# One-hot rows of j built token by token in a two-stage expert kernel

## The chip, the cores and the metric

The kernel runs on one core of a Trainium2 chip. The metric is the device time of one execution in microseconds (us). The engines are named as in the profile: PE is TensorE's matrix multiplication and PEld its weight load, DVE is VectorE, ACT is ScalarE, POOL is GpSimd, and SP issues most of the DMAs.

## What is computed

The reference is one layer on x of shape (2, 4096, 256): an attention-like part with running sums, and then an expert part whose choice of experts is made per token. Cut to the expert part:

```
s1 = einsum('bshd,nd->bshn', q1, K1);  s2 = einsum('bshd,nd->bshn', q2, K2)   # 8 heads, 64 keys each
v1, i1 = top_k(s1, 10);  v2, i2 = top_k(s2, 10)
vals, best = top_k(v1[..., :, None] + v2[..., None, :], 10)                # per head
expert_idx = (i1 * 64 + i2)[best]                                          # 0..4095
scores = softmax(vals)
h = einsum('bsd,bshkd->bshk', x, W_down[expert_idx])
h = gelu(h) * scores
out = einsum('bshk,bshkd->bsd', h, W_up[expert_idx])
```

Each token picks 8 x 10 = 80 experts among the first 4,096, with a weight for each.

## The kernel before, in words

The kernel doesn't gather the experts. It computes gelu(x W_down) for all 4,096 experts, multiplies it by a weight that is zero for an expert that was not picked, and multiplies the result with all of W_up. An expert's number is written as e = 32 j + c, with j from 0 to 127 (JE = 128) and c from 0 to 31 (EC = 32).

The work goes in 32 blocks of 256 tokens (16 stretches of each of the 2 sequences, in turn). A block's work has these parts:

- `attention`: the attention part of a block, with the norms, up to the queries qT.
- `scores` and `route`: for each half block of 128 tokens, the scores, the top 10 of each side and of their sums, the softmax, and the numbers j and c. They are packed into pk (five planes of 128 x 128 bf16: j, c, and three bf16 parts of the weight), and TensorE transposes the planes, so that a row is one of the 80 picks and a column is a token. ScalarE copies the result out of PSUM: plane j into `row`, and the other four into `rows`, each value repeated RUN = 4 times.
- `hidden`: the matmuls of x2T with the tiles wd (loaded by DMA), and on ScalarE their Gelu, which gives the tiles A (128 j x 32 c x 128 tokens).
- `weigh`: for each token, the weights of all 4,096 experts as a product of two one-hot matrices, and A times them. It is described below.
- `outputs`: the matmuls of A with the tiles wu into ps_acc, a norm, and the sum with x.

`weigh` takes 128 tokens in four builds of TS = 32 tokens. `build` makes on VectorE:

- hj, whether pick r of token t has this j. First, once per 128 tokens, `xj` holds j - 8m for m from 0 to 15 (a copy of `row` and four subtractions that double what is there). Then eight comparisons with the constants 0 to 7, of 16 x 32 elements each, fill hj. Its layout is (j, t): the 128 values of one token lie 32 elements apart.
- hc, whether pick r of token t has this c: one comparison of the constant `cols` (0 to 31) with rows, 32 x 32 elements. Its layout is (t, c).
- hw, hc times each of the three parts of the weight, 3 x 32 x 32 elements.

For each token TensorE then loads the token's 128 x 128 slice of hj as weights (`fl.tensor.ld`) and multiplies it with the token's three parts of hw, 32 columns each, into the token's 32 columns of ps_s (`fl.tensor.mm`, three times). The product of 16 tokens fills one of the two ps_s buffers, and VectorE multiplies A by it. Four tokens make one group in the order on TensorE, and behind each group one matmul of `outputs` of the half block before is put in, where there is one.

All engine operations are recorded first and issued later. `together` interleaves the streams (the experts of block n, the routes of block n+1, the attention of block n+2) by the numbers that they yield. `Flow.plan` then puts each engine's operations into a fixed order: it plays the program with a cost for each operation (`Flow.cost`), and takes on each engine the earliest recorded operation whose inputs are there by those costs. For VectorE a comparison with a constant of n bf16 elements costs n/4/0.96 + 68 ns there, and one of two bf16 tensors n/2/0.96 + 68 ns. The engines run these orders, with semaphores for what one needs of another. Since `emit` issues everything, the profile shows one line for nearly all operations: L404, with L403 for the weight loads of the one-hot product and of the transposes of pk and L401 for their matmuls. The tiles' names tell them apart.

Of the kernel before, what the change touches and what calls it, by code (L numbers as in the profile page):

```python
# [12 lines left out]
BF16 = mybir.dt.bfloat16  # L13
U16 = mybir.dt.uint16
AF = mybir.ActivationFunctionType
ALU = mybir.AluOpType
AX = mybir.AxisListType

P = 128
# [7 lines left out]
JE = 128  # L27
EC = NE // JE
R = 80
TS = 32  # L30
# [3 lines left out]
RUN = 4  # L34
# [381 lines left out]
def layer_kernel(  # L416
# [5 lines left out]
    nc = tc.nc  # L422
# [3 lines left out]
    fl = Flow(nc, tc, ctx)  # L426
    for tag, words in (
        ("ph", 512), ("tmp", 512), ("tmp2", 512), ("sinT", 512), ("cosT", 512), ("xn", 512), ("xT", 514), ("kc", 514),
        ("ks", 514), ("bh", 256), ("gate", 256), ("w0", 256), ("bl", 512), ("qT", 1024), ("v", 256), ("iu", 256),
        ("i1", 40), ("i2", 40), ("ci", 108), ("bv", 80), ("bu", 64), ("left", 8), ("right", 8), ("rsd", 2), ("hot", 1080),  # L430
        ("sm", 80), ("ssum", 8), ("ej", 80), ("rest", 80), ("xj", 1024),
    ):
        fl.ring(tag, words)
    for tag, words in (("st1", 6), ("mv1", 2), ("rs1", 1), ("st2", 12), ("mv2", 4), ("rs2", 2), ("x2T", 512),
                       ("s", 1024), ("hj", 2048), ("hw", 1536), ("hc", 512)):
        fl.ring(tag, words, 2)
    for tag, words in (("row", 64), ("rows", 1024), ("A", 4096), ("wd", 1024), ("wu", 1024)):
        fl.ring(tag, words, 3)
    fl.ring("xt", 512, 4)
    fl.ring("o", 256)  # L440
    for tag, words, bufs in (("mm", 512, 3), ("sc", 1024, 1), ("s", 512, 2), ("acc", 512, 1)):
# [3 lines left out]
    const = ctx.enter_context(tc.tile_pool(name="const", bufs=1))  # L445
# [1 line left out]

    ident = const.tile([P, P], F32, name="ident")
    make_identity(nc, ident)
    cols = const.tile([P, EC], BF16, name="cols")  # L450
    nc.gpsimd.iota(cols, pattern=[[1, EC]], base=0, channel_multiplier=0, allow_small_or_imprecise_dtypes=True)
    iota = const.tile([P, NCAND, RUN], BF16, name="iota")
    nc.gpsimd.iota(iota, pattern=[[1, NCAND], [0, RUN]], base=0, channel_multiplier=0,
                   allow_small_or_imprecise_dtypes=True)
# [40 lines left out]
    ps = fl.tile([1, D], F32, "ps_mm")  # L495
# [299 lines left out]
    def route(s):  # L795


        v = fl.tile([P, NH, 2, 16], F32, "v")
# [12 lines left out]
        i = 0  # L811
        while i < TOPK:
            w, n = WIDTHS[i], WIDTHS.count(WIDTHS[i])
# [45 lines left out]
        n = NCAND  # L859
        while n > 1:  # L860
            m = n // 2
# [5 lines left out]
        sm = fl.tile([P, NH, TOPK], F32, "sm")  # L867
        fl.vector.tensor_sub(sm, bv, bv[:, :, 0:1].to_broadcast([P, NH, TOPK]))
        fl.scalar.activation(sm, sm, AF.Exp)
        ssum = fl.tile([P, NH], F32, "ssum")  # L870
# [6 lines left out]
        ej = fl.tile([P, 2, R], U16, "ej")  # L877
# [4 lines left out]
        rest = fl.tile([P, NH, TOPK], F32, "rest")  # L882
# [7 lines left out]
        ps = fl.tile([P, 5, P], BF16, "ps_mm")  # L890
        with fl.group():
            for n in range(5):
                fl.tensor.ld(ps[:, n, :], pk[:, n, :], is_transpose=True)
                fl.tensor.mm(ps[:, n, :], pk[:, n, :], identb, start=True, stop=True, is_transpose=True)
        row = fl.tile([P, P], BF16, "row")
        rows = fl.tile([P, P // TS, 4, TS, RUN], BF16, "rows")
        fl.scalar.copy(row, ps[:, 0, :])
        fl.scalar.copy(rows.rearrange("p q n t u -> p n q t u"), ps[:, 1:5, :].rearrange("p n (q t) -> p n q t", t=TS)
                       .unsqueeze(4).to_broadcast([P, 4, P // TS, TS, RUN]))
        return row, rows  # L900

    def hidden(x2T):

# [31 lines left out]
    def weigh(A, rows, before):  # L935

        row, rows = rows
        xj = fl.tile([P, 16, P], BF16, "xj")  # L940
        fl.vector.tensor_copy(xj[:, 0, :], row)
        for s in (8, 4, 2, 1):
            v = xj.rearrange("r (a b s) t -> r a b s t", b=2, s=s)
            fl.vector.tensor_scalar(v[:, :, 1, 0, :], v[:, :, 0, 0, :], 8.0 * s, None, ALU.subtract)

        yield 3

        def build(t0):
            hj = fl.tile([P, JE, TS], BF16, "hj")
            for i in range(8):  # L950
                fl.vector.tensor_scalar(hj.rearrange("r (m j) t -> r m j t", j=8)[:, :, i, :],
                                        xj[:, :, t0 : t0 + TS], float(i), None, ALU.is_equal)
            hc = fl.tile([P, TS, EC], BF16, "hc")
            fl.vector.tensor_tensor(
                hc.rearrange("r t (a u) -> r t a u", u=RUN),
                cols.rearrange("r (a u) -> r a u", u=RUN).unsqueeze(1).to_broadcast([P, TS, EC // RUN, RUN]),
                rows[:, t0 // TS, 0].unsqueeze(2).to_broadcast([P, TS, EC // RUN, RUN]), ALU.is_equal,
            )
            hw = fl.tile([P, 3, TS, EC], BF16, "hw")
            fl.vector.tensor_mul(  # L960
                hw.rearrange("r n t (a u) -> r n t a u", u=RUN),
                hc.rearrange("r t (a u) -> r t a u", u=RUN).unsqueeze(1).to_broadcast([P, 3, TS, EC // RUN, RUN]),
                rows[:, t0 // TS, 1:4].unsqueeze(3).to_broadcast([P, 3, TS, EC // RUN, RUN]),
            )
            return hj, hw

        ready = build(0)
        yield 3
        for t0 in range(0, P, TS):
            hj, hw = ready  # L970
            if t0 + TS < P:
                ready = build(t0 + TS)
                yield 3
            for g in range(0, TS, TG):
                ps = fl.tile([P, TG, EC], F32, "ps_s")
                for t in range(0, TG, TU):
                    with fl.group():
                        for i in range(t, t + TU):
                            w = hj[:, :, g + i]
                            fl.tensor.ld(ps[:, i, :], w)  # L980
                            for n in range(3):
                                fl.tensor.mm(ps[:, i, :], w, hw[:, n, g + i, :], start=n == 0, stop=n == 2)
                    next(before, None)
                a = A[:, :, t0 + g : t0 + g + TG]
                fl.vector.tensor_mul(a, ps.rearrange("p t c -> p c t"), a)
                yield 1
        for _ in before:
            pass
        yield 1
# [16 lines left out]
    def routes(qT):  # L1006
        rows = []
        for s in scores(qT):
            rows.append((yield from route(s)))
        return rows  # L1010

    def experts(block, xt, A, rows, before, x2T):


        for j in range(NJ):
            yield from weigh(A[j], rows[j], before)
            before = outputs(*block, j, xt, A[j])
        A = None
        if x2T is not None:
            A = yield from hidden(x2T)  # L1020
        return A, before
# [7 lines left out]
    for n, block in enumerate(blocks):  # L1029
# [7 lines left out]
        A, before = ends[0]  # L1037
        x0 = x1
        if not last1:
            rows = ends[1]  # L1040
# [39 lines left out]
```

## Time and profile before

| | us |
|---|---|
| median of 3 runs (least to most) | 4083.58 (4077.91 to 4088.07) |
| the profiled execution | 4087.09 |
| its span, first to last instruction | 4085.3 |
| PE busy (share) | 3834.6 (94%) |
| DVE busy | 3735.9 (91%) |
| ACT busy | 1837.9 (45%) |
| POOL busy | 153.9 (4%) |

The profiled execution is 3.5 us above the median. Busy times of an engine are those of its operations, with overlaps counted once. Matmuls are pipelined, so a busy PE is not PE at its peak. The costliest groups of the product are 24,576 matmuls ps_s<-hw,hj (994.9 us busy), 8,192 weight loads of hj (963.9), 2,048 comparisons for hj (512.0), 256 products hw (446.0), 512 products A<-ps_s,A (346.7) and 256 comparisons hc (171.1). The first weight load of hj is at 194.6 us; before it the first blocks' attention, routes and hidden layer are made.

### The profile page before, as it was taken

The page shows a single profiled execution, that of the slowest core. Times are in us where ns is not written, and L with a number is a line of the kernel's source. Part 1 is how long each engine was busy: PE and PEld are TensorE (multiplying, and loading weights), DVE is VectorE, ACT ScalarE, POOL GpSimd, SP SyncE. Part 2 cuts the span into 40 slices and gives each one's busy share as a digit, 9 for nine tenths or more (in the row PEclk, how much of TensorE's full clock was granted, in tenths as well). Part 3 has the DMA queues.
Part 4 walks back from the last instruction along what each step waited for, and adds up shares of the span by engine and source line. Part 5 has one row for each costly group of instructions (what it writes and reads, how often), then busy time and mean ns, then how long its engine had stood idle before and what let it go on. Part 6 is the DMA issues. An engine that isn't in the chain of part 4 may idle for free.

```text
span 4085.3 us, 79868 instructions
## 1 busy us (share of the span) xinstructions
PE 3834.6 (94%) x36870; PEld 3300.2 (81%) x20486; DVE 3735.9 (91%) x17525; ACT 1837.9 (45%) x3251; POOL 153.9 (4%) x264
## 2 busy tenths in 40 slices
PE   3499999999999999999999999999999999999998
PEld 2388888888888888888888888888888888888887
DVE  3879999999999999999999999999999999999986
ACT  3344544444544444544444544444544444544431
POOL 0000000000000000000000000000000000000000
PEclk8699999999999999999999999999999999999989
DMA  5023333223333233333233333233333233333233
GB/s 205 29 93 120 106 115 123 90 96 127 101 116 125 89 100 124 106 115 123 91 96 127 100 117 125 89 100 124 98 122 122 90 98 126 103 115 125 86 108 121
DMA packets 145151, 447.83 MB, mean 110 GB/s; under 512 B 17777, under 2 KB 44146, under 8 KB 143730
## 3 DMA queue, kind: packets, MB, share of 16 engines
q1 hardware_dynamic: 139392, 440.46, 33.2%
q8 instruction: 225, 3.69, 0.4%
q10 hardware_dynamic: 5362, 2.28, 0.2%
q14 instruction: 172, 1.41, 0.1%
HBM read 425.90 MB, written 16.78 MB: 108 GB/s over the span
## 4 chain that ended last, share of the span: by engine, by line
PE 66%; DVE 31%; ACT 2%; ACTq 1%; issue 1%; DMA 0%; POOL 0%; POOLq 0%; SPq 0%
PE ps_mm L404 35%; PE ps_s L401 16%; PE ps_acc L404 12%; DVE hj L404 6%; DVE hw L404 4%; DVE hot L404 4%; PE ps_sc L404 3%; DVE ph L404 2%; DVE A L404 2%; DVE st L404 1%; DVE iu L404 1%; DVE hc L404 1%; DVE bl L404 1%; DVE v L404 1%; ACT rows L404 1%; DVE bu L404 1%
## 5 line engine op out<-in xcount | busy, mean ns | idle before, releaser
L404 PE MATMUL ps_mm<-x2T,wd 128*128 128x256 f32 x4096 | 1115.9, 423 | 44.2 <-ACT A L404 25.8
L403 PEld LDWEIGHTS <-hj 128*128 128x128 bf16 x8192 | 963.9, 141 | 103.2 <-DVE hw L404 29.0
L404 PEld LDWEIGHTS ps_mm<-x2T,wd 128*128 128x128 f32 x4096 | 854.0, 213 | 214.0 <-issue 81.9
L401 PE MATMUL ps_s<-hw,hj 128*128 128x32 bf16 x24576 | 994.9, 189 | 31.5 <-DVE hj L404 13.8
L404 PE MATMUL ps_acc<-wu,A 128*128 128x256 f32 x4096 | 1006.6, 393 | 6.9 <-DVE o L404 4.2
L404 PEld LDWEIGHTS ps_acc<-wu,A 128*128 128x128 f32 x4096 | 792.4, 197 | 123.5 <-DVE o L404 10.2
L404 ACT ACT_TABLE_LOAD x658 | 844.2, 1283 | 38.8 <-issue 26.0
L404 ACT ACTIVATE A<-ps_mm 128x256 f32<-128x256 f32 x1024 | 349.5, 383 | 976.3 <-PE ps_mm L404 961.3
L404 DVE TENSOR_SCALAR hj<-xj 128x512 bf16<-128x512 bf16 x2048 | 512.0, 302 | 0.0
L404 DVE TENSOR_TENSOR hw<-hc,rows 128x3072 bf16<-128x3072 bf16 x256 | 446.0, 1742 | 0.0
L404 DVE TENSOR_TENSOR A<-ps_s,A 128x512 f32<-128x512 f32 x512 | 346.7, 680 | 102.3 <-PE ps_s L401 62.4
L404 DVE FIND_INDEX8 iu<-v,s 128x8 uint32<-128x64 f32 x2048 | 428.1, 217 | 0.0
L404 DVE MAX8 v<-s 128x8 f32<-128x64 f32 x2048 | 374.3, 210 | 15.9 <-ACT s L404 15.9
L404 ACT ACTIVATE sm<-sm 128x80 f32<-128x80 f32 x64 | 17.3, 270 | 706.7 <-DVE sm L404 706.6
L404 DVE MATCH_REPLACE8 s<-v,s 128x64 f32<-128x64 f32 x1024 | 210.5, 208 | 0.0
L404 POOL CAST pk<-sm 128x80 bf16<-128x80 f32 x64 | 35.6, 556 | 3830.3 <-DVE sm L404 3830.3
L404 DVE TENSOR_TENSOR hc<-cols,rows 128x1024 bf16<-128x1024 bf16 x256 | 171.1, 678 | 0.0
L404 DVE MATCH_VALUE_LOAD iu<-v,s 128x8 f32 x2048 | 149.3, 73 | 0.0
L404 DVE RECIPROCAL rs<-rs 128x2 f32<-128x2 f32 (+1 forms) x160 | 22.3, 154 | 136.5 <-ACT rs L404 136.5
L404 PE MATMUL ps_mm<-x2T,wq 128*128 128x256 f32 x512 | 125.2, 388 | 1.0 <-ACT qT L404 0.6
L404 PE MATMUL ps_sc<-kbd,qT 128*128 128x256 f32 x512 | 124.8, 386 | 0.2 <-ACT qT L404 0.2
L404 PE MATMUL ps_mm<-xT,wg 128*128 128x256 f32 x512 | 122.3, 386 | 0.3 <-ACT tmp L404 0.3
(161 smaller groups left out, 4159.7 us busy)
## 6 DMA issues: line engine op xcount, KB each, us to landing
wu<-wu_d SPq DMA_DIRECT2D x512, 512.0 KB, 4.2
wd<-wd_d SPq DMA_DIRECT2D x256, 512.0 KB, 3.5
xt<-in_attn_x_dram SPq DMA_DIRECT2D x32, 256.0 KB, 2.9
A<-in_table_dram SPq DMA_DIRECT2D x8, 1024.0 KB, 7.2
out_dram<-o SPq DMA_DIRECT2D x64, 128.0 KB, 3.1
ph<-in_attn_pos_phases_dram SPq DMA_DIRECT2D x16, 256.0 KB, 3.9
wu_d<-A SPq DMA_DIRECT2D x8, 512.0 KB, 5.2
wd_d<-wd SPq DMA_DIRECT2D x8, 512.0 KB, 3.3
```

Source lines behind the costliest of these rows:

```text
L401: return engine.add_instruction(ins)
L403: return engine.ldweights(args[1], is_transpose=kw.get("is_transpose"), tile_position=(0, 0))
L404: return getattr(engine, op)(*args, **kw)
```

## The change

hj gets hc's layout, (t, j), so that the 128 values of one token are neighbours. It is made as hc is, by one comparison of two tensors: `cols`, which now counts to 127, against plane j of rows. So `rows` holds all five planes, in one ScalarE copy, and `row`, `xj` and its five operations per 128 tokens are gone. The weight load takes `hj[:, g + i, :]` in place of `hj[:, :, g + i]`. hw, hc, the matmuls and A's product are what they were.

```
-        row = fl.tile([P, P], BF16, "row")
-        rows = fl.tile([P, P // TS, 4, TS, RUN], BF16, "rows")
-        fl.scalar.copy(row, ps[:, 0, :])
-        fl.scalar.copy(rows.rearrange("p q n t u -> p n q t u"), ps[:, 1:5, :].rearrange("p n (q t) -> p n q t", t=TS)
-                       .unsqueeze(4).to_broadcast([P, 4, P // TS, TS, RUN]))
-        return row, rows
+        rows = fl.tile([P, P // TS, 5, TS, RUN], BF16, "rows")
+        fl.scalar.copy(rows.rearrange("p q n t u -> p n q t u"), ps.rearrange("p n (q t) -> p n q t", t=TS)
+                       .unsqueeze(4).to_broadcast([P, 5, P // TS, TS, RUN]))
+        return rows
...
-        row, rows = rows
-        xj = fl.tile([P, 16, P], BF16, "xj")
-        fl.vector.tensor_copy(xj[:, 0, :], row)
-        for s in (8, 4, 2, 1):
-            v = xj.rearrange("r (a b s) t -> r a b s t", b=2, s=s)
-            fl.vector.tensor_scalar(v[:, :, 1, 0, :], v[:, :, 0, 0, :], 8.0 * s, None, ALU.subtract)
-
...
-            hj = fl.tile([P, JE, TS], BF16, "hj")
-            for i in range(8):
-                fl.vector.tensor_scalar(hj.rearrange("r (m j) t -> r m j t", j=8)[:, :, i, :],
-                                        xj[:, :, t0 : t0 + TS], float(i), None, ALU.is_equal)
-            hc = fl.tile([P, TS, EC], BF16, "hc")
-            fl.vector.tensor_tensor(
-                hc.rearrange("r t (a u) -> r t a u", u=RUN),
-                cols.rearrange("r (a u) -> r a u", u=RUN).unsqueeze(1).to_broadcast([P, TS, EC // RUN, RUN]),
-                rows[:, t0 // TS, 0].unsqueeze(2).to_broadcast([P, TS, EC // RUN, RUN]), ALU.is_equal,
-            )
+            def onehot(tag, n, width):
+                h = fl.tile([P, TS, width], BF16, tag)
+                fl.vector.tensor_tensor(
+                    h.rearrange("r t (a u) -> r t a u", u=RUN),
+                    cols[:, 0:width].rearrange("r (a u) -> r a u", u=RUN).unsqueeze(1).to_broadcast([P, TS, width // RUN, RUN]),
+                    rows[:, t0 // TS, n].unsqueeze(2).to_broadcast([P, TS, width // RUN, RUN]), ALU.is_equal,
+                )
+                return h
+
+            hj, hc = onehot("hj", 0, JE), onehot("hc", 1, EC)
...
-                            w = hj[:, :, g + i]
+                            w = hj[:, g + i, :]
```

The constant `cols` is made by an iota of 128 in place of 32 elements, the ring of `rows` grows from 1,024 to 1,280 words, and the rings of `row` and `xj` are gone. The other uses of rows move up by one plane.

## The prediction

> **What bounds the kernel now.** I read the page's busy times and chain first, then the stages, then the single operations of the one-hot product. Part 1 of the page, and the first lines of part 4:
>
> ```profile
> PE 3834.6 (94%) x36870; PEld 3300.2 (81%) x20486; DVE 3735.9 (91%) x17525; ACT 1837.9 (45%) x3251; POOL 153.9 (4%) x264
> ...
> PE 66%; DVE 31%; ACT 2%; ACTq 1%; issue 1%; DMA 0%; POOL 0%; POOLq 0%; SPq 0%
> ```
>
> Two engines are nearly full. The chain runs two thirds through TensorE, so it looks like the bound, but VectorE has hardly more room. The stage view says how much, for the 29 middle blocks (339 to 3895 us; columns: length, busy time of PE, PEld, DVE, ACT, POOL, clock, DMA):
>
> ```profile
> 339.00:3895.00 3556.00, 3440.19 (x33348) 2974.86 (x18499) 3378.51 (x15859) 1669.87 (x2939) 138.18 (x232) 0.94 0.34 109
> ```
>
> A block lasts 3556.0/29 = 122.6 us. VectorE works 116.5 us of it and is idle 6.1. So whatever TensorE gains, a middle block can't fall by more than those 6.1 us, less what VectorE is given in addition. What ends its idle time, in the two blocks from 2056 to 2302 us (the waits of DVE: total, times, longest):
>
> ```profile
> DVE rs L404 <- ACT rs L404: 7.9, 3, 3.0
> DVE A L404 <- PE ps_s L401: 2.5, 5, 0.8
> DVE rsd L404 <- PE ps_mm L404: 1.2, 2, 0.6
> DVE A L404 <- ACT A L404: 0.9, 2, 0.5
> ```
>
> **Part 1, the weights.** The product's operations, from the answers on the tile hj and on the line of the weight loads (ns: least, median, most):
>
> ```profile
> L403 PEld LDWEIGHTS <-hj x8192: 135/143/169, 194.6 to 4060.4; 128*128 128x128 bf16 x200
> L403 PEld LDWEIGHTS <-pk x320: 97/98/152, 144.8 to 4000.8; 128*128 128x128 bf16 x160
> L401 PE MATMUL ps_s<-hw,hj x24576: 176/176/253, 194.6 to 4060.5; 128*128 128x32 bf16 x200
> ```
>
> Both loads take 128x128 bf16 weights. Those of hj lie 32 elements (64 bytes) apart, those of pk are neighbours, as the new hj's will be. The difference is 45 ns. The token's own rhythm shows that these 45 ns are paid: over the 7,800 tokens whose four operations are all recorded, the load starts 2 ns after the matmul before it, the first matmul 23 ns later, the second 60 to 69 ns after that, the third 25 ns after the second. The first matmul takes some 211 to 219 ns where the others take 176: it is held about 40 ns for its weights. The mean is 121.4 ns for a token, as in the chain of waits, where 96 matmuls (32 tokens) last 3.87 us:
>
> ```profile
> 2101.00 3.87 PE ps_s L401 x96
> ```
>
> If the hold goes, a token takes 2 + 23 + 25 + 25 = 75 to 77 ns. The pk row supports it: there a load and a 128-column matmul follow each other every 56 ns at full clock, with no hold (matmul 219 ns, of which about 43 for the 96 more columns). The likeness isn't full, since pk's are transposes. So TensorE saves 8,192 x 45 ns = **369 us, 11.5 us a block**. Bounds: nothing, if the spacing isn't what costs, and 8,192 x 46 = 377.
>
> The Trainium skill, TensorE: Matmul & The Clock Gate, Weight-path perf modes, speaks against this: fast weight load reads the weights in 4 chunks of 32 columns, "packed or strided", for column steps up to 1,024 elements. By that rule a step of 32 costs nothing, the saving on TensorE is zero, and the time that of the second rival below. The recorded operands of both loads have that form (4 groups), yet 143 stands against 98 ns; I go by the rows.
>
> **Part 2, VectorE.** Removed: 8 comparisons per build (2,048 in all), and per 128 tokens one copy and four subtractions for xj (64 times). Added: one comparison of 4,096 elements per build (256). Durations overlap on this engine, so I count from start to start. The timeline of DVE in a stretch without waits:
>
> ```profile
> 2063.76 1.69 DVE L404 TENSOR_SCALAR hj<-xj 128x512 bf16<-128x512 bf16 x8
> 2065.38 1.28 DVE L404 TENSOR_TENSOR hc<-cols,rows 128x1024 bf16<-128x1024 bf16 x2
> 2066.58 1.75 DVE L404 TENSOR_TENSOR hw<-hc,rows 128x3072 bf16<-128x3072 bf16 x1
> 2068.25 0.42 DVE L404 BATCH_NORM_STATS2 st<-ps_acc 128x6 f32<-128x256 f32 x1
> ```
>
> Eight old comparisons cost 1.62 us, one hc 0.60, one hw 1.67. The new one has hc's form with 4,096 elements: between hc and hw an element costs (1.67 - 0.60)/2,048 = 0.522 ns, so 0.60 + 3,072 x 0.522 ns = 2.20 us, dearer by 0.58 than the eight. Over the run: new 256 x 2.20 = 563; old, summed from start to start, 454 (mean 222 ns, since 312 of them fall on POOL's work and average 337 against 201; the TENSOR_TENSOR halvings of hot take 106 and 107 ns with and without POOL, so the new comparison should escape that); xj 54. Net **+55 us, 1.7 us a block**. Bounds: -10 from the page's busy column, which counts overlaps (584 - 512 - 82), and +95 if POOL's delay moves to a neighbour (563 - 414 - 54).
>
> Also lost: 470 of the old comparisons stand alone between two other operations, 15 a block, and fill the place between dependent ones. Without a filler a dependent operation starts 36 ns after the end before it and not 80 ns ahead of it: 0 to 15 x 0.116 = 1.7 us a block; I take half, 0.8.
>
> **Part 3, the rest.** ScalarE's copies row (266 ns) and rows (2,048 elements, 1,871) become one of 2,560. At (1,871 - 266)/1,920 = 0.84 ns an element that is 2.30 us, +0.16 us, 64 times, hidden by ScalarE's 55% idle. TensorE waits for rows 30 times (21.6 us in all), so at worst +5 us; TensorE has that to spare afterwards. The iota is one POOL operation at the start. No DMA and no wait is added; hj waits for rows, made a block earlier. Costs in the planner change (hj 201 x 8 to 2,201 ns), so the order on the engines may shift; blocks 11 and 25, with an order of their own, last 120.3 and 120.1 us instead of 122.6, so this is worth a couple of us in a block, of either sign.
>
> **The sum**, per middle block, on VectorE, which is late next: +1.7 (work) + 0.8 (fillers). Waits for ps_s and for A, 3.4/2 = 1.7: they stand in the stage where TensorE is sped up, so they go. Waits rs and rsd, 9.1/2 = 4.55: one rs wait in two blocks (2.05 us) is nearly all table load and square root behind VectorE's own mv (1.28 + 0.30), so 0.85 a block stays. The other 3.7 come because ScalarE stands behind A<-ps_mm, which waits for TensorE (3.02 us at 2142); they lie in the hidden stage, whose matmuls are not sped up, and shrink only as TensorE enters it earlier. I let half go, 1.85. Net 1.7 + 0.8 - 1.7 - 1.85 = -1.05, times 29 = **-30 us**. The first and the last two blocks (144.8, 106.2 and 83.6 us) have VectorE idle for 30, 11 and 41 us; of their 3 x 11.5 = 34.5 us I count half, **-17**. Span 4085.3 - 47 = 4038; this execution took 4087.1 (1.8 around the span), 3.5 above the median, so in the median's terms 4083.6 - 47 = **4037 us**. Of TensorE's 369 us, some 320 turn into idle.
>
> **Rivals.**
> *VectorE sets the pace and its waits stay.* TensorE's gain lies in stages where VectorE has 1.7 us of idle a block, and the ScalarE waits of the hidden stage stay. For it: VectorE is 39.78 of 40 us busy from 2094 to 2134, just where the product runs. Then +1.7 + 0.8 with nothing back, x 29 = +73, less 17: 4140. It decides once more than 6.1 - 2.5 = 3.6 us of idle a block is left. Against it: a TensorE with 15 us to spare should be late less often.
> *The loads don't get quicker.* TensorE as before; VectorE's 55 us come on top, of which 31% (its share of the chain) to all: 4100 to 4139. Against it: pk.
> *More is given back.* All waits that TensorE causes go (1.7 + 3.7), fillers cost nothing, the edge blocks give all: (1.7 - 5.4) x 29 - 34 = -141: 3942. Against it: TensorE's clock. It is 0.94 in the middle and 0.90 from 2134 to 2167 us, behind waits; with more idle it may drop. At 0.90 throughout TensorE's 107 us become 112, still under VectorE's 118, but bursts behind a wait come late.
>
> **How the numbers follow.** Forecast (4005 to 4070) 0.48; more given back (below 4005) 0.14; gains and costs cancel (4071 to 4096) 0.14; VectorE's pace 0.20; loads no quicker 0.04. About 0.3% (12 us) is what a measurement of this kernel can tell from no change: faster 0.62, within 0.14, slower 0.24. The range leaves about a tenth on each side: 3965 to 4130.
>
> **What will show it.** Right: LDWEIGHTS <-hj near 98 ns; 96 matmuls of ps_s in about 2.5 us; PE's busy time near 3,470 us; hj as x256 near 2.28 us; DVE at some 118 us a block and the larger part of the chain; waits of A for ps_s near zero. Wrong: hj loads still near 143; an hj comparison beyond 2.3 us; waits rs and rsd still above 3.6 us a block, or a clock well below 0.90.

## The result and the profile after

| | before | after |
|---|---|---|
| median of 4 runs each, run side by side (us) | 4081.25 | 4295.41 (4290.46 to 4296.3) |
| ratio, 95% interval | | 1.052 [1.0502, 1.0538] |
| profiled execution, its span (us) | 4087.09, 4085.3 | 4290.46, 4288.7 |
| granted clock of TensorE, mean | 0.929 | 0.911 |

The kernel is 5.2% slower, where 1.1% faster was forecast, and outside the range. Page, part 1 and the first line of part 4, after:

```profile
PE 3535.6 (82%) x36870; PEld 2955.2 (69%) x20486; DVE 3783.9 (88%) x15413; ACT 1848.6 (43%) x3184; POOL 276.2 (6%) x264
...
DVE 45%; PE 39%; ACT 10%; POOL 4%; issue 1%; ACTq 1%; DMA 0%; POOLq 0%; SPq 0%
```

TensorE has 299 us less to do, VectorE only 48 more, and yet both shares fell: each engine waits more. POOL's busy time rose by 122 us with the same 264 instructions, and POOL and ACT stand in the chain with 14%, where they had 2%. The stage view of the 29 middle blocks, after (columns as before):

```profile
332.80:4094.50 3761.70, 3176.17 (x33350) 2665.94 (x18501) 3421.19 (x13947) 1681.95 (x2879) 249.91 (x232) 0.92 0.31 103
```

A block lasts 129.7 us (before: 122.6). VectorE works 118.0 of it and is idle 11.7 (before: 116.5 and 6.1). So 5.6 of the 7.1 us are new idle time of VectorE. The operations of the tile hj, after:

```profile
L403 PEld LDWEIGHTS <-hj x8192: 95/96/152, 188.6 to 4263.6; 128*128 128x128 bf16 x200
L404 DVE TENSOR_TENSOR hj<-cols,rows x256: 2257/2282/2318, 166.2 to 4251.4; 128x4096 bf16<-128x4096 bf16 x128
```

The load fell from 143 to 96 ns. The most common token takes 75 ns from load to load (2 + 23 + 25 + 25); the mean, 85.5 (before: 121.4), has waits in it. The comparison has a median of 2.28 us and costs 2.20 from start to start (562.9 us for 256). What the change does to these operations is what was forecast. What it does to the waits isn't. Waits of DVE over the whole run (total us, times, longest), before and then after. rs and rsd are reciprocals that the norms and the attention need, v is the top-10 search, and ph and xn are made in the attention:

```profile
DVE rs L404 <- ACT rs L404: 136.5, 50, 22.3
DVE A L404 <- PE ps_s L401: 62.4, 87, 4.5
DVE A L404 <- ACT A L404: 39.0, 30, 25.4
DVE rsd L404 <- PE ps_mm L404: 22.0, 32, 3.5
```

```profile
DVE A L404 <- PE ps_s L401: 165.6, 52, 4.5
DVE rs L404 <- ACT rs L404: 122.8, 35, 22.5
DVE v L404 <- ACT s L404: 58.9, 32, 9.0
DVE A L404 <- ACT A L404: 49.9, 32, 25.8
DVE ph L404 <- PE ps_mm L404: 38.9, 32, 5.1
```

The wait that was to go, A for ps_s, rose from 62.4 to 165.6 us, although its matmuls have become faster. What TensorE waits for, after:

```profile
PE ps_mm L404 <- DVE xn L404: 177.3, 32, 6.0
PE ps_mm L404 <- DVE ph L404: 150.1, 33, 33.8
PE ps_mm L401 <- POOL pk L404: 143.9, 60, 4.3
PE ps_s L401 <- DVE A L404: 61.4, 51, 4.1
```

Before, the first two were 38.2 and 37.2 us, and the third, the transposes of pk that wait for POOL, was not among its seven longest (the seventh was 13.8). TensorE stands still there, with the next product behind it in its queue, so VectorE then waits for ps_s. POOL's last three operations on pk split the routing weight into its bf16 parts; their groups, before and after (columns: busy us, mean ns, idle before):

```profile
L404 POOL TENSOR_TENSOR pk<-rest,pk 128x80 bf16<-128x80 f32 x64 | 42.0, 657 | 5.1
...
L404 POOL TENSOR_TENSOR rest<-sm,pk 128x80 f32<-128x80 f32 x64 | 31.6, 494 | 5.1
```

```profile
L404 POOL TENSOR_TENSOR rest<-sm,pk 128x80 f32<-128x80 f32 x64 | 121.3, 1895 | 5.1
L404 POOL TENSOR_TENSOR pk<-rest,pk 128x80 bf16<-128x80 f32 x64 | 70.3, 1098 | 5.1
```

The same subtraction takes 494 ns before and 1,895 after. The timeline of POOL's two subtractions and of DVE in one block of after shows what lies beside them:

```profile
2096.50 3.05 POOL L404 TENSOR_TENSOR rest<-sm,pk 128x80 f32<-128x80 f32 x1
...
2100.51 1.65 POOL L404 TENSOR_TENSOR pk<-rest,pk 128x80 bf16<-128x80 f32 x1
```

```profile
2096.41 2.29 DVE L404 TENSOR_TENSOR hj<-cols,rows 128x4096 bf16<-128x4096 bf16 x1
2098.61 0.69 DVE L404 TENSOR_TENSOR hc<-cols,rows 128x1024 bf16<-128x1024 bf16 x1
...
2100.02 1.73 DVE L404 TENSOR_TENSOR hw<-hc,rows 128x3072 bf16<-128x3072 bf16 x1
```

The subtraction begins just after hj's comparison does, and ends at 2099.55, a quarter of a microsecond after hc's. The other one, begun at 2100.51 inside hw, ends at 2102.16, after hw. Both look held while VectorE works on two bf16 tensors, and end soon after it.

### The profile page after: what moved, and what is told of

Read it like the earlier page. It is cut to its first block, busy times and chain, and to the rows that moved or that the text cites. A ratio compares the mean times of both kernels' runs of the same rounds, so it can differ in the third digit from the quotient of the medians.

```text
span 4288.7 us, 77762 instructions
## 1 busy us (share of the span) xinstructions
PE 3535.6 (82%) x36870; PEld 2955.2 (69%) x20486; DVE 3783.9 (88%) x15413; ACT 1848.6 (43%) x3184; POOL 276.2 (6%) x264
## 3 DMA queue, kind: packets, MB, share of 16 engines
q10 hardware_dynamic: 5362, 2.28, 0.2%
## 4 chain that ended last, share of the span: by engine, by line
DVE 45%; PE 39%; ACT 10%; POOL 4%; issue 1%; ACTq 1%; DMA 0%; POOLq 0%; SPq 0%
PE ps_mm L404 27%; PE ps_acc L404 9%; DVE hj L404 7%; DVE hw L404 6%; DVE hot L404 6%; DVE A L404 5%; ACT L404 4%; DVE iu L404 4%; DVE v L404 2%; POOL pk L404 2%; POOL rest L404 2%; DVE ph L404 2%; DVE hc L404 2%; DVE s L404 2%; DVE st L404 2%; ACT rows L404 2%
## 5 line engine op out<-in xcount | busy, mean ns | idle before, releaser
L404 PE MATMUL ps_mm<-x2T,wd 128*128 128x256 f32 x4096 | 1081.8, 413 | 173.9 <-DVE ph L404 112.7
L404 PEld LDWEIGHTS ps_mm<-x2T,wd 128*128 128x128 f32 x4096 | 836.0, 208 | 330.7 <-issue 204.9
L404 PE MATMUL ps_acc<-wu,A 128*128 128x256 f32 x4096 | 962.0, 383 | 5.8 <-DVE o L404 2.4
L404 PEld LDWEIGHTS ps_acc<-wu,A 128*128 128x128 f32 x4096 | 766.9, 190 | 113.4 <-DVE A L404 7.9
L404 ACT ACTIVATE A<-ps_mm 128x256 f32<-128x256 f32 x1024 | 343.5, 382 | 1088.1 <-PE ps_mm L404 1071.0
L403 PEld LDWEIGHTS <-hj 128*128 128x128 bf16 x8192 | 636.6, 97 | 179.2 <-DVE A L404 89.2
L401 PE MATMUL ps_s<-hw,hj 128*128 128x32 bf16 x24576 | 685.3, 178 | 72.4 <-DVE A L404 61.4
L404 DVE TENSOR_TENSOR hj<-cols,rows 128x4096 bf16<-128x4096 bf16 x256 | 584.2, 2282 | 0.0
L404 DVE TENSOR_TENSOR A<-ps_s,A 128x512 f32<-128x512 f32 x512 | 344.7, 679 | 215.6 <-PE ps_s L401 165.6
L404 DVE TENSOR_TENSOR hw<-hc,rows 128x3072 bf16<-128x3072 bf16 x256 | 445.6, 1741 | 0.0
L404 DVE FIND_INDEX8 iu<-v,s 128x8 uint32<-128x64 f32 x2048 | 429.4, 218 | 0.0
L404 DVE MAX8 v<-s 128x8 f32<-128x64 f32 x2048 | 371.6, 212 | 58.9 <-ACT s L404 58.9
L404 ACT ACTIVATE sm<-sm 128x80 f32<-128x80 f32 x64 | 17.2, 269 | 724.7 <-DVE sm L404 724.3
L404 POOL CAST pk<-sm 128x80 bf16<-128x80 f32 x64 | 39.0, 610 | 3924.5 <-DVE sm L404 3924.5
L404 DVE MATCH_REPLACE8 s<-v,s 128x64 f32<-128x64 f32 x1024 | 211.2, 209 | 0.0
L404 PE MATMUL ps_mm<-ident,xn 128*128 128x128 f32 x256 | 56.4, 357 | 178.4 <-DVE xn L404 177.3
L404 ACT COPY rows<-ps_mm 128x2560 bf16<-128x2560 bf16 x64 | 146.1, 2283 | 132.7 <-PE ps_mm L401 132.7
L404 DVE TENSOR_TENSOR hc<-cols,rows 128x1024 bf16<-128x1024 bf16 x256 | 173.4, 678 | 1.2 <-ACT rows L404 1.2
L404 PEld LDWEIGHTS ps_mm<-ident,xn 128*128 128x128 f32 x256 | 37.5, 174 | 188.6 <-DVE xn L404 183.5
L401 PE MATMUL ps_mm<-identb,pk 128*128 128x128 bf16 x320 | 32.9, 243 | 156.4 <-POOL pk L404 143.9
L404 DVE MATCH_VALUE_LOAD iu<-v,s 128x8 f32 x2048 | 152.6, 74 | 0.0
```

The lines of the kernel that those rows point to most:

```text
L401: return engine.add_instruction(ins)
L403: return engine.ldweights(args[1], is_transpose=kw.get("is_transpose"), tile_position=(0, 0))
L404: return getattr(engine, op)(*args, **kw)
```

## The experiments

Three theories, and the names for them here. **V**: VectorE sets the pace, and its added work counts almost in full (the first rival). **P**: the long comparison holds POOL, TensorE waits for pk, VectorE for TensorE. **O**: the new costs and the new steps give the planner another order, and that order is worse.

To take O apart from the rest, some kernels have the planner order steps that are then not issued ("planned only"). So a kernel can have one kernel's operations in the other's order on every engine. In these, profile lines L401, L403 and L404 become L420, L422 and L423.

The ledger that the readings below rest on. VectorE's work is its busy time with overlaps counted once, its idle time what is left between its first and its last operation, both in the profiled execution. Each ratio is to the runs of the kernel before beside that kernel, whose median was 4080 to 4091; differences in us are taken from 4081, so those to the kernel before are good to some 10 us:

| kernel | median us | ratio to before | VectorE's work | its idle |
|---|---|---|---|---|
| before (profiled run) | 4081 | 1 | 3735.6 | 343.7 |
| after | 4295.41 | 1.052 [1.0502, 1.0538] | 3783.6 | 499.0 |
| e1 new operations, old order | 4187.70 | 1.0274 [1.0214, 1.0333] | 3835.5 | 344.2 |
| e2 old operations, new order | 4277.36 | 1.0493 [1.0432, 1.0553] | 3722.9 | 546.3 |
| e3 after, POOL's work out | 4187.25 | 1.0273 [1.0213, 1.0333] | 3769.1 | 408.0 |
| e4 e1, POOL's work out | 4079.67 | 0.9994 [0.9972, 1.0017] | 3819.6 | 250.8 |
| e5 before, POOL's work out | 3989.95 | 0.9752 [0.9718, 0.9787] | 3685.4 | 301.2 |
| e6 after, measured costs | 4416.45 | 1.0803 [1.0767, 1.0839] | 3789.6 | 612.6 |
| e7 before, measured costs | 4491.02 | 1.0984 [1.0947, 1.1020] | 3730.1 | 754.0 |
| e8 e1, half the comparison | 3952.31 | 0.9699 [0.9635, 0.9764] | 3564.8 | 379.7 |
| e9 e1, 1.5 comparisons | 4440.49 | 1.0897 [1.0827, 1.0968] | 4118.1 | 319.2 |
| e10 before, split off POOL | 4090.15 | 1.0005 [0.9970, 1.0040] | 3728.1 | 355.4 |
| e11 before, eight as one | 4145.12 | 1.0176 [1.0110, 1.0242] | 3744.8 | 391.2 |
| e12 before, weights 4 apart | 3977.24 | 0.9735 [0.9717, 0.9753] | 3726.2 | 241.9 |
| e13 before, weights 8 apart | 4086.56 | 1.0011 [0.9999, 1.0024] | 3734.9 | 342.0 |
| e14 e2, old charge | 4349.39 | 1.0645 [1.0622, 1.0667] | 3743.5 | 598.3 |
| e15 before, weights 2 apart | 4146.62 | 1.0170 [1.0127, 1.0213] | 3899.3 | 230.7 |
| e16 e1, comparison in eight | 4242.93 | 1.0382 [1.0350, 1.0413] | 3918.3 | 316.3 |

### Operations and order taken apart: e1, e2

e1 plans the old steps and issues the new operations at their places (the whole comparison where the eighth old one stood):

```
             for i in range(8):
-                fl.vector.tensor_scalar(hj.rearrange(...)[:, :, i, :], xj[:, :, t0 : t0 + TS], float(i), None, ALU.is_equal)
+                fl.add("vector", "tensor_scalar", (...), {}, real=[whole] if i == 7 else (), ...)
```

> The changed kernel's operations, but every engine's order as in the kernel before: the plan is made with the old operations and their costs, and the one new comparison is issued at the place of the last of the eight old ones. Theory O (the planner's new costs gave another order, and that order waits more): the new operations are worth what was forecast, 4040 us (3990 to 4080). Theory P (the new comparison holds up POOL's work on pk while it runs, and TensorE waits for pk in its order): the contention depends on what stands beside POOL, in the old order the comparison stands there too, so 4150 to 4300. Theory V (VectorE's longer work sets the pace): 4100 to 4150.

e2 is the other corner: the new kernel's plan, with `real=eight`, the eight old comparisons in a row at the place of the new one, and with the old layout.

> The operations of the kernel before, but every engine's order as in the changed kernel: the plan is made with the one new comparison and its cost, and the eight old comparisons are issued at its place; xj and row are charged nothing. Theory O: the order alone costs the time, so 4290 us or more, since the slow weight loads come on top (4290 to 4400). Theory P: POOL isn't held up by the old comparisons, so 4080 to 4150.

The four corners: 4081 (old, old), 4188 (new operations, old order), 4277 (old operations, new order), 4295 (both). In the old order the new operations cost 107 us; the new order costs the old operations 197, and the new ones 108. e1's time lies in P's range and 38 us above V's; e2's is 13 us short of O's and far above P's. So both sides, the operations and O, hold a part, and the parts don't add up: in the new order the operations cost only 18, since VectorE has idle time there that TensorE's gain can shorten (546 to 499).

In e1 VectorE works 100 us more, and its idle time is what it was (344). Its waits and TensorE's:

```profile
DVE A L423 <- PE ps_s L420: 105.6, 51, 3.2
DVE rs L423 <- ACT rs L423: 56.0, 20, 21.9
DVE A L423 <- ACT A L423: 47.5, 31, 23.9
DVE rsd L423 <- PE ps_mm L423: 39.7, 32, 3.5
```

```profile
PE ps_mm L420 <- POOL pk L423: 131.0, 60, 3.9
PE ps_s L420 <- DVE A L423: 100.2, 67, 4.4
PE ps_mm L423 <- DVE xn L423: 95.7, 31, 6.0
PE ps_mm L423 <- DVE hot L423: 94.5, 30, 3.4
```

rs went from 136.5 to 56.0, as hoped. But ps_s rose by 43 and rsd by 18, and TensorE waits 131 us for POOL, in the old order too. So P's stall doesn't need the new order. ScalarE's longer copy of rows shows no such part: TensorE waits 17.3 us for rows, before 21.6.

### POOL's part: e3, e4, e5, e10, e16

e3 (after), e4 (e1) and e5 (before) issue only the first of the four operations of the split; the other three are planned only:

```
         fl.gpsimd.tensor_copy(parts[0], sm)
-        fl.gpsimd.tensor_sub(rest, sm, parts[0])
+        fl.add("gpsimd", "tensor_sub", (rest, sm, parts[0]), {}, real=())
...
```

> The changed kernel in its own order, without three of POOL's four operations for each half block (rest, and the second and third part of the weight, so that the weights keep only their first bf16 part). Theory P: without the work that is held up, TensorE's waits for pk (143.9 us in the changed kernel) and what follows from them go: 4295 - 144 = 4150 us or less. Theory O: the other waits of that order stay: 4250 to 4295.

> The changed kernel's operations in the old order, as in the first experiment (4188 us), and three of POOL's four operations for each half block left out (the weights keep only their first bf16 part). Theory P, by which the new comparison holds POOL up and TensorE waits behind pk: the 131 us of TensorE's waits for POOL go, 4188 - 131 = 4057 us, within 4030 to 4090. Theory V, by which VectorE's longer work alone sets the pace in the old order: 4150 to 4188.

> The kernel before in its own order with the same three operations of POOL left out, a control. Theory P: TensorE hardly waits for POOL there, so the time stays within 1%, 4050 to 4085; the old comparisons that fall on POOL's work lose their delay of 42 us on VectorE. If POOL's work costs the kernel before as much as the changed one, about 3960.

Without POOL's work each kernel gains about the same: after 108, e1 108, before 91 to 101. e3's time lies between the ranges of P and O, e4's in P's range, e5's between the two that were named. e4 alone would have looked like proof of P: it is as fast as the kernel before (0.9994), and its wait for ps_s is nearly gone (in e3 it falls from 165.6 to 47.3 us). e4's waits of A, and then e5's:

```profile
DVE A L423 <- ACT A L423: 49.1, 30, 24.9
...
DVE A L423 <- PE ps_s L420: 12.7, 19, 2.6
```

```profile
DVE A L423 <- PE ps_s L420: 75.0, 94, 4.6
DVE A L423 <- ACT A L423: 36.1, 19, 26.5
```

The control e5 forbids the reading that P is all. The kernel before gains too, in another way: its old comparisons are no longer delayed by POOL (453.9 to 413.4 us for the 2,048) and 43 us of its idle time go. Between e4 and e5, with POOL out of both, the new operations still cost 90 us (4079.7 to 3990.0): VectorE's work +134, its idle -50. P as the cause of the whole difference falls. What stays of it is that in e1 POOL's work is worth 93 us of VectorE's idle time, against 43 in the kernel before.

e10 gives the split to ScalarE and VectorE in the kernel before, at the old places, with POOL's steps planned only:

```
+        fl.add("scalar", "copy", (parts[0], sm), {}, charge=free)
+        fl.add("vector", "tensor_sub", (rest, sm, parts[0]), {}, charge=free)
...
```

> The kernel before, in nearly its own order (one in 250 of TensorE's operations changes its place), with the weight's three parts made by two copies on ScalarE and two subtractions on VectorE in place of four operations on POOL. If POOL's work costs the kernel before 100 us, as its leaving out showed (3990), then 3990 + 64 x 2 x 0.15 us = 4010, within 3985 to 4040. If the steps between ScalarE and VectorE take as long as POOL did: 4070 to 4100.

1.0005: no gain, as expected if the steps back and forth take as long as POOL did. VectorE's old comparisons are free of POOL, but the split costs it two operations for each half block, and its idle time is 12 us more. e16 keeps the split on POOL and cuts the new comparison into eight pieces of 4 tokens, at the eight old places:

```
-                       real=[whole] if i == 7 else (), ...)
+                       real=[four], also=[rows[:, t0 // TS, 0]])     # hj[:, 4*i : 4*i+4, :] of the same comparison
```

> The changed kernel's layout in the old order (4188 us), with the new comparison cut into eight of 4 tokens each, 512 elements, at the very places of the eight old ones. By the line through hc and hw a piece costs 0.33 us, 2.67 a build and not 2.20: 120 us more for VectorE, less what the pieces fill between dependent operations (46 us). Theory P (an unbroken run of the new comparison holds POOL, and TensorE's waits behind pk take back the quick load's gain): POOL's rest falls from 1.6 us back to some 0.5, TensorE no longer waits for pk, VectorE's idle time falls from 344 to about 250: 4188 + 74 - 94 = 4168, within 4140 to 4200. Without that: 4188 + 74 = 4262, within 4230 to 4310.

4243, 55 us slower than e1. hj costs 694 us (+133 for the eight starts), VectorE's idle falls by 28, and TensorE waits 95.1 us for pk, in 31 places in place of 60. Where POOL's subtraction met a row of pieces it was still held (30 of 64 took 3.3 to 3.4 us), where VectorE did something else in between it wasn't (29 took 0.5). This backs the hold itself, but the time lies in the range that was stated for no gain from POOL's release, not in P's. As a test of the price it is only half a release.

### VectorE's part: e8, e9

In e1's order, e8 makes only j < 64 of hj (the other half stays zero, so half the experts get no weight), and e9 makes the first half a second time into a spare tile:

```
-                hj.rearrange("r t (a u) -> r t a u", u=RUN), ...
+                hj.rearrange("r t (a u) -> r t a u", u=RUN)[:, :, 0 : JE // RUN // 2], ...
```

> The changed kernel's operations in the old order (4188 us), with the new comparison made for j below 64 only (2,048 elements; picks with a larger j get no weight). By the line through hc and hw it costs 1.13 us in place of 2.20, so VectorE has 256 x 1.07 = 274 us less to do. Theory V (in this order every us of VectorE's work counts in full, and TensorE's gain is worth nothing beside it): 4188 - 274 = 3914, within 3890 to 3960. Theory P (POOL's delay and TensorE's waits behind it set the time): the comparison still holds POOL, though for half as long, 4050 to 4140.

> The same operations in the old order, with one more comparison of 2,048 elements into a tile that nobody reads, behind each new one: 256 x 1.13 = 289 us more for VectorE. Theory V: 4188 + 289 = 4477, within 4440 to 4500. Theory P: VectorE's idle time of 344 us takes in a part of it, 4250 to 4420.

e8: 235 us faster than e1 for 271 us less work. e9: 253 slower for 283 more. A microsecond of VectorE's work is worth 0.87 to 0.89 us of time, both ways from e1. Both times lie in V's ranges (e9 at its lower end) and outside P's, so V holds: here VectorE sets the pace. POOL's hold changes along, though (its subtraction takes 1,113 ns in e8, 1,613 in e1 and 2,141 in e9), so a part of that price may be POOL's.

### The order: e11, e6, e7, e14

e11 is the kernel before with one edit: the eight comparisons are one step for the planner, with the sum of their costs.

```
+            with fl.group():
                 for i in range(8):
```

> The kernel before, with its own operations and its own costs, but the eight comparisons of a build planned as one step in place of eight. Theory G (the order is worse because the plan can't put single comparisons between other work any more): most of the 197 us that the new order alone cost, 4200 to 4300. Theory C (it is the changed cost, or the order is accidental): 4060 to 4140.

1.0176, 4145 us: just above the range of theory C and below that of G. On VectorE's ledger +9 of work and +48 of idle time. So some 57 of the 197 us come from planning one long step in place of eight short ones. e6 and e7 test whether the plan was bad because its costs of TensorE are wrong. They set the measured ones, in after and before:

```
             if op in ("mm", "ld"):
-                return 26.0, 200.0
+                return (25.0 if op == "mm" else 1.0), 176.0       # e7: 46.0 for ld
-            return elems(outs[0]) * 4 / 2.4 + 10, elems(outs[0]) * 4 / 2.4 + 190
+            return elems(outs[0]) * 2 / 2.4 + 2, elems(outs[0]) * 2 / 2.4 + 166
```

(The costs of `transpose` likewise: 109 and 275 in place of 70 and 240.)

> The changed kernel, with the planner's costs for TensorE set to the measured spacing (216 ns and 380 to the result for a 256-column f32 matmul in place of 437 and 617; 109 for a transpose; 25 for a matmul and 1 for a weight load of the one-hot product). Theory O in the form that the order is bad because the plan takes TensorE for twice as slow as it is and so takes VectorE's results for early: 3950 to 4150. If the order is only accidental: 4150 to 4350.

> The kernel before with the same measured costs (46 for the weight load, so that a token takes 121 ns). If the plan's wrong costs for TensorE were harmful in general, it is faster too: 3950 to 4060. If the kernel before had an order that happened to fit: 4080 to 4250.

Truer costs give worse orders, by 121 and 410 us, beyond every range that was named, so that theory falls. e14 is e2 with the one step charged what the eight were, 8 x 201 ns, in place of 2,201:

```
-            ), {}, real=eight, also=[xj[:, :, t0 : t0 + TS]])
+            ), {}, real=eight, also=[xj[:, :, t0 : t0 + TS]], charge=(8 * 201.3, 8 * 201.3 + 92))
```

> The second experiment again (the old operations, planned in the changed kernel's steps, 4277 us), but the one step for hj is charged 1,610 ns as eight old comparisons were, and not 2,201. If the higher charge makes the bad order: 4145, as with the eight planned as one in the kernel before. If it is the steps (one comparison, no xj, one copy of rows): 4250 to 4290.

72 us slower than e2, and outside both ranges, where the old charge was to help or to change little. The time is no smooth function of what the planner is told. What in the new order costs the rest of the 197 us stays open.

### The weights' layout by itself: e12, e13, e15

These are the kernel before, with its comparisons, its costs and its order. Only the place of an element in hj changes, so that a token's weights lie 4, 8 or 2 elements apart and not 32:

```
-            hj = fl.tile([P, JE, TS], BF16, "hj")
+            hj = fl.tile([P, TS // 4, JE, 4], BF16, "hj")
...
-                            w = hj[:, :, g + i]
+                            w = hj[:, (g + i) // 4, :, (g + i) % 4]
```

> The kernel before with its own comparisons, costs and order, but hj laid out so that the 128 weights of a token are 4 elements apart in place of 32 (groups of 4 tokens are innermost). The load alone, without the dearer comparison. If the load's time depends on the step down to neighbours, and VectorE's comparisons in runs of 4 stay at 202 ns: the waits of VectorE for TensorE go as they did without POOL's work (93 us), 3990, within 3960 to 4040. If TensorE's gain is worth nothing because VectorE sets the pace: 4070 to 4090. If runs of 4 make the comparisons slower (302 ns or more): 4150 and above.

> The same with the weights 8 elements (16 bytes) apart. If the load is quick for any step below 32: as with a step of 4. If only near neighbours load quickly: LDWEIGHTS at 143 ns and 4080.

> As with the step of 4 (3977 us, load 112 ns, a token about 87 ns), but the weights are 2 elements apart and the comparisons run in pieces of 2. If the load gets quicker still (about 98 ns, a token 76 ns) and the comparisons stay at 202 ns: VectorE's idle time is 242 us already, most of it not for the product, so 3960 to 3977. If pieces of 2 slow the comparisons, at 302 ns or more: 4080 and above.

The loads of hj in e12, e13 and e15, in this order:

```profile
L403 PEld LDWEIGHTS <-hj x8192: 110/113/152, 192.5 to 3947.8; 128*128 128x128 bf16 x200
```

```profile
L403 PEld LDWEIGHTS <-hj x8192: 140/143/167, 191.3 to 4058.2; 128*128 128x128 bf16 x200
```

```profile
L403 PEld LDWEIGHTS <-hj x8192: 96/97/152, 191.3 to 4110.3; 128*128 128x128 bf16 x200
```

A step of 8 changes neither load nor time (1.0011), as for "only near neighbours". A step of 4 gives 113 ns and a most common token of 87, and the time falls to **3977 us, 0.9735 [0.9717, 0.9753]**: faster than both kernels. A step of 2 gives 97 ns, but its comparisons, with pairs as their shortest runs, cost 633 us in place of 454, and it is slower than the kernel before. VectorE in e12, page and waits:

```profile
PE 3553.6 (89%) x36870; PEld 2994.6 (75%) x20486; DVE 3726.6 (94%) x17525; ACT 1839.9 (46%) x3251; POOL 152.7 (4%) x264
...
DVE 59%; PE 37%; ACT 3%; issue 1%; ACTq 0%; DMA 0%; POOL 0%; POOLq 0%; SPq 0%
```

```profile
DVE A L404 <- ACT A L404: 59.7, 32, 25.4
DVE rs L404 <- ACT rs L404: 58.8, 25, 22.7
DVE rsd L404 <- PE ps_mm L404: 22.0, 32, 3.5
DVE A L404 <- PE ps_s L401: 18.3, 20, 2.7
```

With VectorE's work as it was, the waits for ps_s and rs go from 62.4 and 136.5 to 18.3 and 58.8, and its idle time falls by 102 us. The chain has turned over to VectorE without a loss.

## Why the prediction was wrong

**The weights: right, but their worth on TensorE mis-sized.** 96 ns where 98 was forecast, 75 ns a token, at the low end of 75 to 77. The steps 2 to 32 confirm that it is the spacing. But the 45 ns a token set a mean with waits in it (121.4) against a rhythm without (75 to 77); the prediction's own starts, 2 + 23 + 60 to 69 + 25, make 110 to 119. The means went from 121.4 to 85.5, 36 ns, which is 294 us and not 369. PE's busy time agrees: it fell by 299, to 3,536, not 3,470. As TensorE had most of that to spare, this is not what failed.

**The marks that were to show it** were nearly all met: 96 ns, hj as x256 at 2.28 us, VectorE at 118.0 us a block and the larger part of the chain (45%). They are marks of work. Only the waits of A for ps_s, to be near zero, told of the loss. None of the signs of being wrong came, either: rs kept 97.9/29 = 3.4 us a block in the middle of after, just below the 3.6 named. New waits came beside it, v and ph, 2.5 a block. The first and last blocks gave 2 us of the 17 counted on (the stretch before the middle ones is 6 us shorter, that behind them 4 longer).

**What TensorE's gain is worth by itself: right in total, with luck.** The sum let (1.7 + 1.85) x 29 = 103 us of VectorE's waits go, 49 of them waits of A and 54 of rs and rsd. e12 is the quick load with VectorE's work left alone, and there 102 us of idle time went, with 87 ns a token and not 75. But the waits of A fell only by 23 (101.4 to 78.0), and those of rs and rsd by 78 (158.5 to 80.8). The two misses cancel.

**The comparison: right.** 2.20 us from start to start, as worked out; net +53.5 us in e1 against +55.

**The fillers: mis-sized.** Half of at most 1.7 us a block was taken, 0.8. In e1 VectorE's other operations cost 46 us more, 1.6 a block: about the bound, not its half. They are mostly small dependent ones (the 128 copies of iu go from 15.6 to 26.3 us). In e16, where eight pieces stand at the old places again, these 46 us are gone (work +183 against before, of it hj and xj +186).

**"They stand in the stage where TensorE is sped up, so they go": the first step that failed.** In the kernel as changed they grew, in the old order too (e1: for ps_s from 62.4 to 105.6, all waits of A from 101.4 to 153.1, up 52 where 49 were to go). rs and rsd fell by 63, more than the 54 counted on; VectorE's gaps of under 0.15 us, before dependent operations, grew by 11. So of its idle time as a whole, 0 of the 103 us came back in e1. What held the waits of A is shown: POOL's split is held by the long comparison, and TensorE stands 131 us before pk. With the split out of both kernels, the waits of A do fall by 49, from 111.1 (e5) to 61.8 (e4). In idle time, the split's removal is worth 93 us in e1 and 43 in the kernel before, so some 50 of the 103 us are POOL's. The prediction had seen POOL and VectorE slow each other (337 against 201 ns), asked only what this does to VectorE, and wrote that "the new comparison should escape that". It did; POOL didn't. The other part, by e4 against e5, is rs and rsd: without POOL they fall by 11 and not by 54. That is the first rival, with 0.20 the largest chance after the forecast's: "VectorE sets the pace and its waits stay". It gave 4140; e1 has 4188. Its point of decision was 3.6 us of idle a block left. The stage view of e1's middle:

```profile
332.00:4000.00 3668.00, 3201.26 (x33374) 2682.68 (x18526) 3474.93 (x13964) 1679.27 (x2884) 285.72 (x234) 0.92 0.32 106
```

Its blocks follow each other every 126.2 us, and VectorE is idle for (3668.0 - 3474.9)/3668.0 x 126.2 = 6.6 of it (before: 6.1). So nothing of the idle time went. And e8 and e9 show the price of VectorE's work in this order: nearly one for one. Of 100 us more work and nothing back, 107 us follow.

**"A couple of us in a block, of either sign": the second step that failed, by size.** The basis was two blocks that stood in another order and differed by 2.4 us. The new order costs 197/29 = 6.8 us a block with the old operations and 108/29 = 3.7 with the new ones. That is half of the whole loss of 214 us, and more than the gain that was forecast. Two blocks of one plan say little about another plan: a single step in place of eight cost 2 us a block (e11). Why the new order is worse beyond that stays open.

**The sum as measured**, from the run of before: operations in the old order +107 (VectorE's work +100, its idle time 0; the other 7 lie within the spread of before), the order +108: 4081 + 215 = 4296.

## What to carry to other kernels

When two engines are both above 90%, a gain on one that is paid for on the other has to be compared at the other's price; look for the form of the change that leaves the second engine's instructions as they are (here a step of 4 took the mean token from 121.4 to 93.9 ns, where a step of 1 gave 85.5, at no cost on VectorE). Where a planner orders the instructions, a change of an operation's length or count changes every order, so hold the order fixed in one experiment before the operations are blamed. And where the profile shows two engines slowing each other, price both directions, and run the same omission on the kernel before as a control.

## What the runs showed of the hardware

**Load time and the spacing of the weights.** 128x128 bf16 weights load in 96 ns at a step of 1 element, 97 at 2, 113 at 4, 143 at 8 and 143 at 32; the median from one token's load to the next is 75, 75, 87, 118 and 117 ns. The Trainium skill (TensorE: Matmul & The Clock Gate, Weight-path perf modes) gives the read pattern of the fast weight load as 4 chunks of 32 columns, "packed or strided". What the prediction weighed as following from it, that a step costs nothing, holds here for a step of 2 and for none from 4 on.

**POOL beside VectorE.** A subtraction of 128x80 on POOL took 0.4 to 0.8 us beside other work and 3.05 beside the new comparisons of two bf16 tensors; these weren't slowed (at most 2,318 ns, median 2,282). Eight old comparisons in a row, followed by hc, held it too in e2 (mean 1,575 ns, 2.4 us beside them). In the kernel before (494) and in e11 (460), where the eight are planned as one step, POOL wasn't held, and in the kernel before the comparisons were the slower ones (337 ns beside POOL against 201). What decides which engine is held, the runs leave open. The Trainium skill, GPSIMD Engine Reference, Specifications, says that POOL shares its SBUF interfaces with VectorE and contends with VectorE's instructions that have two inputs in SBUF or run in a 2-port perf mode. The timeline of after agrees on the first kind, and adds that a POOL operation may be held for the whole length of two such instructions in a row.

**Short runs in a comparison with a constant.** With runs of 4 elements or more the 512-element comparison has a median of 282 to 284 ns, with runs of 2 (e15) it has 402.

**The clock.** TensorE's mean granted clock was 0.946 in e12 (PE 89% busy), 0.929 before (94%), and 0.911 in after (82%) and e1 (85%). So it doesn't follow the busy share alone; by what it goes, no run here tells.
